# Graph attention with layer norm: another order for the last blocks' normalisation, and a flag read without its bounds check

## The chip, the cores and the metric

The kernel runs on one core of one Trainium2 chip. The metric is the device time of one execution in microseconds. Each time given for a kernel is the median of several executions; a profiled execution adds a trace with the start and length of every instruction, the events of every semaphore and the packets of the DMA engines.

## The reference

The inputs are x (4096 rows of 512 float32), a dense adjacency matrix adj (4096 x 4096 float32, 64 MiB), W (512 x 2048: four heads of 512 columns) and a (4 heads x 1024). The reference computes (`h` is x, `N` is 4096)

```python
ht = (h @ W).reshape(N, N_HEADS, N_HIDDEN).transpose(1, 0, 2)
src = jnp.einsum('hnd,hd->hn', ht, a_src)
dst = jnp.einsum('hnd,hd->hn', ht, a_dst)
e = jax.nn.leaky_relu(src[:, :, None] + dst[:, None, :], SLOPE) + adj_mat[None]
att = jax.nn.softmax(e, axis=-1)
h_prime = jnp.einsum('hij,hjd->hid', att, ht)
return h_prime.mean(axis=0)
...
x = _layernorm(x + _L0_gnn_ref(x, adj, L0_gnn_W, L0_gnn_a), axis=-1)
```

The entries of adj that are not zero are uniform up to 1e9, so the largest entry of a row outweighs all others in the softmax: the attention of row i is 1 at the column of the largest adj value and 0 elsewhere. The result for that row is then layernorm(x[i] + x[j] @ mean over heads of W), with j that column.

## The kernel before, in words

The kernel takes that short way for all rows (`leading_rows`), counts the rows for which a bound doesn't prove that the short way is exact, and branches to a full computation (`general`) where the count is above zero. On these inputs the branch is not taken.

**Tiling.** The 4096 rows are 32 blocks of 128 (`NB = 32`, blocks 0 to 31). With `Q = 4`, `LATE` is 28 and `BEHIND` is 24, so `LATE - 1` is block 27, and `NB - 3`, `NB - 2`, `NB - 1` are 29, 30 and 31. For each block SyncE's queue loads 2 MiB of adj into one of six buffers. VectorE reduces it to maxima of segments of 16 or 32 columns (L169), finds the largest segment (L176, L178), GpSimd fetches that segment again by an indirect DMA (L191), VectorE finds the place in it (L214), and GpSimd gathers the row of x with that number (L202). TensorE turns the gathered block (L229), ScalarE copies it out of PSUM into `yt` (L231, `turn`), and TensorE multiplies with the mean of W's heads (L244, `products`).

**Normalisation.** There are two ways. Blocks 0 to 26 use ScalarE and GpSimd: `stats` makes mean and sum of squares with two ScalarE passes (L266, L268), `rstd` makes the factors with three small GpSimd instructions (L271 to L273), and `finish` applies them on ScalarE (L277). Blocks 27 to 31 use VectorE: `moments` (L297, L301, and a square root on ScalarE, L303), `factor` (a reciprocal on VectorE, L306, and with `shift` one instruction more, L308), and `normalise` (L313) on VectorE; block 27 is applied by `finish` on ScalarE, and block 31 half by VectorE and half by ScalarE.

**Blocks 24 to 27** have their x loaded late. Their product is put aside by ScalarE (`put_by`) in one adj buffer, and x is added later by `add_x`: on GpSimd for 24, 25 and 26, on VectorE for 27.

**Order.** The schedule is written out by hand: each engine runs its instructions in the order of the Python calls. The loop over `t` does the 32 blocks; everything after the loop (L479 to L542) is the tail that the change touches. Stores are issued there, all on SyncE's queue, in the order in which the code names them: SyncE waits for the block of each store before it issues it, and then goes to the next. The sixteen stores use eight DMA semaphores in turn. The last six are 28, 29, the pair 24 and 25, the pair 26 and 27, 30, and 31 (L540 to L542). Stored blocks are 256 KiB each.

**The end.** `report` writes the number of unproven rows to `any_bad`; every engine loads it into a register (L63), and branches (L64). SyncE does so after its last store, and there two instructions more belong to L63: FUSED_REGOPS and SEQ_ASSERT, the check of the value against its bounds. After the branch SyncE waits for the semaphores of all engines and DMAs (L691), the last store's among them, and the program ends.

Of the kernel before, what the change touches and what calls it, by code (L numbers as in the profile page):

```python
# [27 lines left out]
@with_exitstack  # L28
def gat_resnorm_kernel(
    ctx: ExitStack,  # L30
    tc: tile.TileContext,
    x: bass.AP,
    adj: bass.AP,
    W: bass.AP,
    a: bass.AP,
    out: bass.AP,
):

    nc = tc.nc
    N, D = x.shape
    H = a.shape[0]
    KB = D // P  # L50
    NB = N // P

    ctx.enter_context(tc.manual_schedule())

    keep = ctx.enter_context(tc.tile_pool(name="keep", bufs=1))
    ident = keep.tile([P, P], F32, name="ident")
    v = keep.tile([P, KB, 2 * H], F32, name="v")
    n_bad = keep.tile([1, NB], I32, name="n_bad")
    any_bad = keep.tile([1, 1], I32, name="any_bad")

    leading_rows(tc, x, adj, W, a, out, ident, v, n_bad, any_bad)

    flag = nc.values_load(any_bad[0:1, 0:1], min_val=0, max_val=N)  # L63
    with tc.If(flag > 0, preferred_fallthrough_block=True, label="general"):  # L64
        general(tc, x, adj, W, out, ident, v, n_bad)

# [2 lines left out]
def leading_rows(ctx, tc, x, adj, W, a, out, ident, v, n_bad, any_bad):  # L69
# [8 lines left out]
    nc = tc.nc  # L78
    N, D = x.shape
    H = a.shape[0]  # L80
    KB, NB, S = D // P, N // P, N // E
# [4 lines left out]
    LATE = NB - Q  # L86
    BEHIND = LATE - Q
# [6 lines left out]
    rows = ctx.enter_context(tc.tile_pool(name="rows", bufs=2))  # L94
# [112 lines left out]
    def find_inner(ib):  # L207
        nc.vector.max(out=inner[:, ib, :], in_=lead_of[ib])
# [30 lines left out]
    def products(ib, lo=0, hi=KB):  # L239
        start = ib not in o_ps  # L240
        if start:
            o_ps[ib] = psum.tile([P, D], F32, name="o")
        for kb in range(lo, hi):
            nc.tensor.matmul(  # L244
                o_ps[ib], yt_of[ib][:, kb, :], w_sum[:, kb, :],
                start=(start and kb == 0), stop=(kb == KB - 1),
            )
# [11 lines left out]
    def add_x(engine, ib):  # L259
        o = o_ps[ib] = o_ps["by"][:, ib - BEHIND, :]  # L260
        engine.tensor_add(o, o, hold[:, ib, :])

    def stats(ib):
        o, i = o_ps[ib], slice(ib, ib + 1)
        sq = rows.tile([P, D], F32, name="sq")
        nc.scalar.activation(sq, o, AF.Identity, scale=-1.0 / D, accum_out=nm[:, i])  # L266
        sq = rows.tile([P, D], F32, name="sq")
        nc.scalar.activation(sq, o, AF.Square, bias=nm[:, i], accum_out=sd[:, i])  # L268

    def rstd(i):  # L270
        nc.gpsimd.tensor_scalar(sd[:, i], sd[:, i], 1.0 / D, EPS, op0=OP.mult, op1=OP.add)  # L271
        nc.gpsimd.tensor_tensor(sd[:, i], sd[:, i], power[:, : i.stop - i.start], op=OP.pow)  # L272
        nc.gpsimd.tensor_mul(nm[:, i], nm[:, i], sd[:, i])  # L273

    def finish(ib):
        i = slice(ib, ib + 1)
        nc.scalar.activation(hold[:, ib, :], o_ps.pop(ib), AF.Identity, bias=nm[:, i], scale=sd[:, i])  # L277
# [6 lines left out]
    def products_of_half(ib, k):  # L284
        for kb in range(KB):
            nc.tensor.matmul(  # L286
                o_ps[ib][k], yt_of[ib][:, kb, :], w_sum[:, kb, ts(k, D // 2)],
                start=False, stop=(kb == KB - 1),
            )
# [3 lines left out]
    def moments(ib):  # L293

        if ib < NB - 1:
            st = small.tile([P, nc.vector.BN_STATS_DIM], F32, name="st", bufs=2)
            nc.vector.bn_stats(st, o_ps[ib])  # L297
        else:
            st = halves_st
        mv = mean_var[ib] = small.tile([P, nc.vector.BN_AGGR_DIM], F32, name="mv", bufs=3)  # L300
        nc.vector.bn_aggr(mv, st)  # L301
        r = rt[ib] = sd[:, ib : ib + 1]
        nc.scalar.activation(r, mv[:, 1:2], AF.Sqrt, bias=eps)  # L303

    def factor(ib, shift=False):
        nc.vector.reciprocal(rt[ib], rt[ib])  # L306
        if shift:
            nc.vector.scalar_tensor_tensor(  # L308
                nm[:, ib : ib + 1], mean_var[ib][:, 0:1], -1.0, rt[ib], op0=OP.mult, op1=OP.mult
            )  # L310

    def normalise(ib, o, columns=slice(0, D)):
        nc.vector.tensor_scalar(  # L313
            hold[:, ib, columns], o, mean_var[ib][:, 0:1], rt[ib], op0=OP.subtract, op1=OP.mult
        )
# [3 lines left out]
    def stats_of_half(ib, k):  # L319
        nc.vector.bn_stats(halves_st[:, k, :], o_ps[ib][k])  # L320

    def finish_in_halves(ib):

        halves, i = o_ps.pop(ib), slice(ib, ib + 1)
        normalise(ib, halves[0], slice(0, D // 2))
        nc.scalar.activation(hold[:, ib, D // 2 :], halves[1], AF.Identity, bias=nm[:, i], scale=sd[:, i])

    def store(queue, lo, n):
        queue.dma_start(out_rows[:, ds(lo, n), :], hold[:, ds(lo, n), :])
# [82 lines left out]
    def report(pg):  # L412
        nc.vector.tensor_scalar(n_bad, pg, -1.0, float(P), op0=OP.mult, op1=OP.add)
        total = once.tile([1, 1], F32, name="total")
        nc.vector.tensor_reduce(total, pg, axis=AX.X, op=OP.add)
        nc.vector.tensor_scalar(any_bad, total, -1.0, float(N), op0=OP.mult, op1=OP.add)
# [6 lines left out]
    for t in range(NB):  # L423
# [29 lines left out]
        ib = t - PROJECT  # L453
# [48 lines left out]
    stats(BEHIND + 1)  # L502
    factor(LATE)
    normalise(LATE, o_ps.pop(LATE))
    for ib in range(BEHIND, NB):
        find_inner(ib)
    bound(3)
    test()
    turn(NB - 2)
    stats(BEHIND + 2)  # L510
    rstd(slice(BEHIND, BEHIND + 3))
    products(NB - 3, KB - 1, KB)
    pg = count()
    products(NB - 2, 0, KB - 1)
    report(pg)
    moments(NB - 3)
    factor(NB - 3)
    normalise(NB - 3, o_ps.pop(NB - 3))
    turn(NB - 1)
    products(NB - 2, KB - 1, KB)  # L520
    add_x(nc.vector, LATE - 1)
    finish(BEHIND)
    finish(BEHIND + 1)
    moments(LATE - 1)
    finish(BEHIND + 2)
    products_of_half(NB - 1, 0)
    products_of_half(NB - 1, 1)
    nc.vector.tensor_add(hold[:, NB - 2, :], o_ps[NB - 2], hold[:, NB - 2, :])
    o_ps[NB - 2] = hold[:, NB - 2, :]
    moments(NB - 2)  # L530
    factor(LATE - 1, shift=True)
    finish(LATE - 1)
    stats_of_half(NB - 1, 0)
    factor(NB - 2)
    normalise(NB - 2, o_ps.pop(NB - 2))
# [1 line left out]
    moments(NB - 1)  # L537
    factor(NB - 1, shift=True)
    finish_in_halves(NB - 1)
    for ib, n in ((NB - 4, 1), (NB - 3, 1), (BEHIND, 2), (BEHIND + 2, 2), (NB - 2, 1)):  # L540
        store(nc.sync, ib, n)
    store(nc.sync, NB - 1, 1)  # L542

# [152 lines left out]
```

## Time and profile before

| | us |
|---|---|
| median of the three runs shown | 235.62 (235.44 to 236.22) |
| the profiled execution, its own time | 236.22 |
| its span in the trace | 234.7 |
| VectorE busy | 192.2 (82%) |
| TensorE busy | 200.7 (86%) |
| ScalarE busy | 111.7 (48%) |
| GpSimd busy | 100.7 (43%) |
| mean rate of all DMA | 414 GB/s, 97.06 MB |

The profiled execution is the slowest of the three, and 1.5 us of its time lie outside the span. Times within the trace are counted from the start of the span. A line of the timeline gives start, length, engine, source line, operation and shapes, and in brackets how long the engine was idle ahead of it and what ended that. A line of the chain gives start, length and what the end of the program waited for. A line of the windows gives the stretch, its length, then the busy time and number of instructions of TensorE, its weight loads, VectorE, ScalarE and GpSimd, the granted clock, the mean busy share of the core's sixteen DMA engines, and the rate of all of them.

The tail of the trace, in the order of the code (start of each, us):

| block | statistics done | applied | store issued |
|---|---|---|---|
| 28 | 216.28 | 216.98 to 217.79 | 218.20 |
| 29 | 221.42 | 221.98 to 222.79 | 222.82 |
| 24, 25 | 218.21 | 224.61 to 226.13 | 226.16 |
| 26 | 221.09 | 226.22 to 227.02 | 227.94, with 27 |
| 27 | 224.34 | 227.11 to 227.91 | 227.94, with 26 |
| 30 | 226.63 | 227.44 to 227.99 | 228.36 |
| 31 | 229.20 | 229.84 to 230.52 | 230.54 |

### The profile page before, as it was taken

The numbers are of one execution on the slowest core, as the hardware profiler recorded it, in microseconds if no ns is written. First come the engines' busy times: TensorE is split into PE (matmuls) and PEld (weight loads), VectorE is DVE, ScalarE is ACT, GpSimd is POOL, SyncE is SP. The second block draws the span as 40 slices with busy tenths as digits, with TensorE's granted clock in tenths as the row PEclk, the third lists the DMA queues.
The fourth block names the chain that finished last, engine by engine and source line by source line (L and its number), as shares of the span: only waits on it lengthen the run. The fifth ranks groups of instructions, "written<-read, shape, count | busy, mean of one in ns | idle before, by whom it ended". The sixth has DMA issues, their size and how long they took to land.

```text
span 234.7 us, 2494 instructions
## 1 busy us (share of the span) xinstructions
PE 200.7 (86%) x683; PEld 103.0 (44%) x683; DVE 192.2 (82%) x302; ACT 111.7 (48%) x267; POOL 100.7 (43%) x212
## 2 busy tenths in 40 slices
PE   0099859999999999999969979789987988999980
PEld 0034514765656555555525424244433442444360
DVE  2726975669969996999689998998699999989871
ACT  2002112255574647474747464646464555187561
POOL 2022142414626463546444555564364554457400
PEclk9999877999999999999997999979997999999998
DMA  6999999999999999999999999999999999999994
GB/s 233 423 409 430 431 429 415 430 426 425 431 431 421 426 428 428 438 418 436 421 437 431 419 434 422 434 417 435 422 436 413 422 426 423 413 425 420 414 374 197
DMA packets 13697, 97.06 MB, mean 414 GB/s; under 512 B 2152, under 2 KB 2664, under 8 KB 7792
## 3 DMA queue, kind: packets, MB, share of 16 engines
q1 hardware_dynamic: 10080, 88.08, 89.0%
q0 software_dynamic: 3584, 8.77, 9.5%
q8 instruction: 6, 0.10, 0.2%
q14 instruction: 11, 0.09, 0.1%
q10 hardware_dynamic: 16, 0.02, 0.0%
HBM read 88.47 MB, written 8.39 MB: 413 GB/s over the span
## 4 chain that ended last, share of the span: by engine, by line
DMA 48%; POOL 19%; issue 17%; DVE 11%; PE 2%; ACT 0%; POOLq 0%; SPq 0%; DVEq 0%
DMA adj_t<-in_adj_dram 42%; DVE seg L169 8%; POOL y L202 6%; POOL lead L191 5%; DMA y<-in_x_dram,col 3%; DMA lead<-in_adj_dram,row 2%; POOL sd L272 2%; PE o L286 2%; DVE col L222 1%; POOL row L185 1%; POOL start L198 1%; POOL col L216 1%; POOL lead_early L191 1%; DVE at L178 1%; DVE top L176 1%
## 5 line engine op out<-in xcount | busy, mean ns | idle before, releaser
L169 DVE TENSOR_REDUCE seg<-adj_t 128x128 f32<-128x2048 f32 (+3 forms) x68 | 145.9, 2148 | 29.5 <-DMA adj_t<-in_adj_dram 29.4
L244 PE MATMUL o<-w_sum,yt 128*128 128x512 f32 x248 | 116.8, 612 | 0.7 <-ACT yt L231 0.7
L244 PEld LDWEIGHTS o<-w_sum,yt 128*128 128x128 f32 x248 | 45.6, 195 | 55.7 <-issue 44.4
L231 ACT COPY yt<-tp 128x512 f32<-128x512 f32 x32 | 18.8, 588 | 44.4 <-PE tp L229 44.3
L202 POOL DMA_INDIRECT y<-in_x_dram,col x32 | 30.9, 964 | 16.5 <-POOL col L216 15.8
L334 PE MATMUL o<-hold,ident 128*128 128x512 f32 x32 | 21.1, 822 | 15.1 <-POOL row L185 11.5
L237 PE MATMUL o<-hold,ident 128*128 128x512 f32 x52 | 29.0, 645 | 0.0
L229 PE MATMUL tp<-ident,y 128*128 128x128 f32 x128 | 20.0, 280 | 9.2 <-DMA y<-in_x_dram,col 9.1
L185 POOL TENSOR_TENSOR row<-at,first 128x1 uint32<-128x1 uint32 x32 | 6.1, 190 | 43.9 <-DVE at L178 43.6
L229 PEld LDWEIGHTS tp<-ident,y 128*128 128x128 f32 x128 | 14.8, 142 | 21.9 <-issue 20.3
L352 ACT COPY wt<-tp 128x512 f32<-128x512 f32 x16 | 9.2, 587 | 31.5 <-PE tp L350 31.5
L191 POOL DMA_INDIRECT lead_early<-in_adj_dram,row x18 | 18.2, 1010 | 8.8 <-POOL row L185 8.8
L216 POOL TENSOR_TENSOR col<-start,within 128x1 uint32<-128x1 uint32 x31 | 5.9, 189 | 36.5 <-DVE within L214 36.5
L251 ACT ACTIVATE sq<-hold 128x512 f32<-128x512 f32 x32 | 19.8, 619 | 0.0
L358 PEld LDWEIGHTS pv<-at_d,wt 128*128 128x128 f32 x128 | 16.3, 191 | 6.8 <-ACT wt L352 3.7
L334 PEld LDWEIGHTS o<-hold,ident 128*128 128x128 f32 x32 | 8.0, 260 | 25.7 <-POOL row L185 11.5
L335 ACT ACTIVATE w_sum<-o 128x512 f32<-128x512 f32 x4 | 2.4, 598 | 33.6 <-PE o L334 33.6
L277 ACT ACTIVATE hold<-o,nm,sd 128x512 f32<-128x512 f32 x24 | 17.2, 771 | 0.0
L191 POOL DMA_INDIRECT lead<-in_adj_dram,row x14 | 14.1, 1006 | 6.9 <-POOL row L185 6.9
L268 ACT ACTIVATE sq<-o,nm 128x512 f32<-128x512 f32 x24 | 16.5, 688 | 0.8
L358 PE MATMUL pv<-at_d,wt 128*128 128x2 f32 x128 | 15.3, 244 | 0.6 <-ACT wt L352 0.6
L266 ACT ACTIVATE sq<-o 128x512 f32<-128x512 f32 x24 | 14.6, 608 | 0.0
(91 smaller groups left out, 151.4 us busy)
## 6 DMA issues: line engine op xcount, KB each, us to landing
adj_t<-in_adj_dram SPq DMA_DIRECT2D x27, 2048.0 KB
hold<-in_x_dram SPq DMA_DIRECT2D x7, 1024.0 KB
adj_t<-in_adj_dram SPq DMA_DIRECT2D x6, 1024.0 KB
out_dram<-hold SPq DMA_DIRECT2D x10, 512.0 KB
adj_t<-in_adj_dram SPq DMA_DIRECT2D x8, 512.0 KB
hold<-in_L_gnn_W_dram SPq DMA_DIRECT2D x4, 1024.0 KB
out_dram<-hold SPq DMA_DIRECT2D x2, 1024.0 KB
hold<-in_x_dram SPq DMA_DIRECT2D x2, 512.0 KB
```

The costliest lines, as they stand in the source:

```text
L169: nc.vector.tensor_reduce(seg_of[ib][:, ts(k, N // e // n)], adj_t[ib][:, ts(k, N // n)].rearrange("p (s e) -> p s e", e=e), axis=AX.X, op ...
L191: nc.gpsimd.indirect_dma_start(out=lead, out_offset=None, in_=adj_segs_early if early else adj_segs, in_offset=bass.IndirectOffsetOnAxis(a ...
L202: nc.gpsimd.indirect_dma_start(out=y, out_offset=None, in_=x, in_offset=bass.IndirectOffsetOnAxis(ap=col[:, :1], axis=0),)
L229: nc.tensor.transpose(tp[:, kb, :], y[:, ts(kb, P)], ident)
L231: nc.scalar.copy(yt, tp)
L237: nc.tensor.matmul(o_ps[ib], ident, hold[:, ib, :], start=start, stop=False)
L244: nc.tensor.matmul(o_ps[ib], yt_of[ib][:, kb, :], w_sum[:, kb, :], start=(start and kb == 0), stop=(kb == KB - 1),)
L251: nc.scalar.activation(sq, hold[:, ib, :], AF.Square, accum_out=xx[:, ib : ib + 1])
L268: nc.scalar.activation(sq, o, AF.Square, bias=nm[:, i], accum_out=sd[:, i])
L277: nc.scalar.activation(hold[:, ib, :], o_ps.pop(ib), AF.Identity, bias=nm[:, i], scale=sd[:, i])
L334: nc.tensor.matmul(o, ident, hold[:, w_at + kb * H + h, :], start=(h == 0), stop=(h == H - 1))
L358: nc.tensor.matmul(pv[:, kb, h : 2 * H : H], wt[:, k, :], at_d[:, k, h : 2 * H : H], start=(k == 0), stop=(k == KB - 1),)
```

## The change

The flag is read with `skip_runtime_bounds_check_because`, so that FUSED_REGOPS and SEQ_ASSERT go. In the tail, the factors of 24 and 25 (`rstd`) get three GpSimd instructions of their own, issued ahead of 26's; `finish` of 24 and 25 comes ahead of 29's square root on ScalarE, `finish` of 26 behind that root, and all of it ahead of the copy of 31's turned rows. On VectorE, 27 gets its x and its moments ahead of 29's `factor` and `normalise`, and its own `factor` right behind them; `finish` of 27 comes right behind 31's copy. The pair 24 and 25 is stored ahead of 29.

```diff
-    flag = nc.values_load(any_bad[0:1, 0:1], min_val=0, max_val=N)
+    flag = nc.values_load(
+        any_bad[0:1, 0:1], min_val=0, max_val=N,
+        skip_runtime_bounds_check_because="it is N less a count of at most N rows, and only compared with zero",
+    )
...
     normalise(LATE, o_ps.pop(LATE))
+    rstd(slice(BEHIND, BEHIND + 2))
     for ib in range(BEHIND, NB):
         find_inner(ib)
     bound(3)
     test()
     turn(NB - 2)
     stats(BEHIND + 2)
-    rstd(slice(BEHIND, BEHIND + 3))
+    rstd(slice(BEHIND + 2, BEHIND + 3))
     products(NB - 3, KB - 1, KB)
     pg = count()
     products(NB - 2, 0, KB - 1)
     report(pg)
+    finish(BEHIND)
+    finish(BEHIND + 1)
     moments(NB - 3)
+    finish(BEHIND + 2)
+    add_x(nc.vector, LATE - 1)
+    moments(LATE - 1)
     factor(NB - 3)
     normalise(NB - 3, o_ps.pop(NB - 3))
     turn(NB - 1)
     products(NB - 2, KB - 1, KB)
-    add_x(nc.vector, LATE - 1)
-    finish(BEHIND)
-    finish(BEHIND + 1)
-    moments(LATE - 1)
-    finish(BEHIND + 2)
     products_of_half(NB - 1, 0)
     products_of_half(NB - 1, 1)
+    factor(LATE - 1, shift=True)
+    finish(LATE - 1)
     nc.vector.tensor_add(hold[:, NB - 2, :], o_ps[NB - 2], hold[:, NB - 2, :])
     o_ps[NB - 2] = hold[:, NB - 2, :]
     moments(NB - 2)
-    factor(LATE - 1, shift=True)
-    finish(LATE - 1)
     stats_of_half(NB - 1, 0)
...
-    for ib, n in ((NB - 4, 1), (NB - 3, 1), (BEHIND, 2), (BEHIND + 2, 2), (NB - 2, 1)):
+    for ib, n in ((NB - 4, 1), (BEHIND, 2), (NB - 3, 1), (BEHIND + 2, 2), (NB - 2, 1)):
         store(nc.sync, ib, n)
```

## The prediction

> **What bounds the kernel now.** I read the page's slices first. The sixteen DMA engines are busy in every slice but the first and the last, so the kernel is bound by bytes moved, and an order of the tail can gain only what the last slices lose.
>
> ```profile
> span 234.7 us, 2494 instructions
> ...
> DMA  6999999999999999999999999999999999999994
> GB/s 233 423 409 430 431 429 415 430 426 425 431 431 421 426 428 428 438 418 436 421 437 431 419 434 422 434 417 435 422 436 413 422 426 423 413 425 420 414 374 197
> ...
> q8 instruction: 6, 0.10, 0.2%
> ```
>
> Second, the chain of waits over the tail. What ends the compute is 31's gather, which lands at 223.33 after 7.2 us, then its transposes, its products (3.55 us), and half a block's moments and normalisation, ending at 230.52. None of these is a store or a normalisation of 24 to 27.
>
> ```profile
> 216.13 7.20 DMA y<-in_x_dram,col
> ...
> 223.47 0.63 PE tp L229 x4
> ...
> 224.95 3.55 PE o L286 x16
> ...
> 228.53 0.44 DVE halves_st L320
> ...
> 229.96 0.56 ACT hold L326
> ```
>
> Third, SyncE's own waits from 220 us on: what it waits for at the very end.
>
> ```profile
> SPq L329 <- DVE hold L313: 5.0, 2, 3.4
> ...
> SPq L691 <- DMA out_dram<-hold: 0.9, 1, 0.9
> ```
>
> The last wait is on the last store: SyncE comes to it at about 232.8 and goes on at 233.74. The store was issued at 230.54. Fourth, what moves in the meantime, in windows of half a microsecond:
>
> ```profile
> 230.50:231.00 0.50, 0.00 (x0) 0.00 (x0) 0.00 (x0) 0.02 (x1) 0.00 (x0) 1.00 0.62 238
> 231.00:231.50 0.50, 0.00 (x0) 0.00 (x0) 0.00 (x0) 0.00 (x0) 0.00 (x0) 1.00 0.41 160
> 231.50:232.00 0.50, 0.00 (x0) 0.00 (x0) 0.00 (x0) 0.00 (x0) 0.00 (x0) 1.00 1.02 397
> 232.00:232.50 0.50, 0.00 (x0) 0.00 (x0) 0.00 (x0) 0.00 (x0) 0.00 (x0) 0.98 0.22 78
> 232.50:233.00 0.50, 0.00 (x0) 0.00 (x0) 0.00 (x0) 0.00 (x0) 0.00 (x0) 0.50 0.06 25
> ```
>
> The last two columns are the DMA share and the rate. At full load sixteen engines move some 421 GB/s, 26 each; 25 GB/s with a share of 0.06 is one engine working alone. The others ran dry between 230.5 and 231.5 and were done with the last store at 232.2. The semaphore events say the same: of the last store's sixteen increments fifteen come from 232.38 to 232.70, the sixteenth at 233.72; of block 30's, fifteen by 231.82 and one at 232.80. By the packets this late engine closes its share of a store at 228.00, 228.65, 229.29, 230.54, 231.79, 232.43 and 233.08: 0.65 us for a store of 256 KiB, 1.25 for one of 512, with nothing between. It never waits for a store to be issued, it has a backlog. So the program's end is that one engine's queue, and the compute is ahead of it: the other engines began 31's packets at 231.38, 0.83 us after the issue, the late one at 232.44. The compute chain could be 1.06 us later at no cost.
>
> **The change part by part.** Sums are against the profiled execution (span 234.7, own time 236.22). It is the slowest of the three runs; the median is 0.60 lower, and I carry the difference over to it.
>
> ScalarE. After 26's statistics it has 2.4 us of wait around one square root:
>
> ```profile
> 220.90 0.19 ACT L268 ACTIVATION_READ_ACCUMULATOR sq<-adj_t,nm 128x1 f32 x1
> 221.46 0.29 ACT L303 ACTIVATE sd<-mv,eps 128x1 f32<-128x1 f32 x1 [0.37 <-DVE mv L301]
> 224.13 0.59 ACT L231 COPY yt<-tp 128x512 f32<-128x512 f32 x1 [2.38 <-PE tp L229]
> 224.61 1.52 ACT L277 ACTIVATE hold<-adj_t,nm,sd 128x512 f32<-128x512 f32 x2
> ```
>
> After the change: `finish` of 24 and 25 from 221.0 to 222.5 (the pair's 1.52), 29's root to 222.7, `finish` of 26 to 223.4 (0.80), 27's root to 223.6 (0.28, issued 0.2 after). 31's copy can then start at 223.5; its transposes let it start at 224.13. What is queued behind the new work is that copy, and TensorE's last sixteen products wait for it; cover 0.6 us. `finish` of 27 follows the copy, 224.6 to 225.4.
>
> GpSimd. The split factors are three instructions more: 0.19 + 0.72 + 0.20, with gaps 1.3 us. 24's and 25's run from 218.4 (end of 26's x) to 219.7, hidden in GpSimd's wait of 2.8 us for 26's statistics. 26's still start at 221.18 and end by 222.5, ahead of their `finish`. Nothing else is queued behind them but the flag.
>
> VectorE. 29's moments end at 221.42; 27's x (0.68), moments (0.69 + 0.18) then run to 223.06 where 29's reciprocal (0.16) and normalisation (0.81) were; these end at 224.1 instead of 222.79, and 27's factors (0.16 + 0.16) at 224.4.
>
> ```profile
> 222.71 0.68 DVE L261 TENSOR_TENSOR adj_t<-adj_t,hold 128x512 f32<-128x512 f32 x1
> 223.43 0.69 DVE L297 BATCH_NORM_STATS2 st<-adj_t 128x6 f32<-128x512 f32 x1
> 224.99 0.69 DVE L528 TENSOR_TENSOR hold<-o,hold 128x512 f32<-128x512 f32 x1 [0.66 <-PE o L244]
> ```
>
> Block 30's addition waits for TensorE until 224.99 as before: 0.5 us of cover are left. Behind it 27's two factor instructions are gone, some 0.26, so 30 is normalised at 227.85 instead of 227.99, with half of 31 still ending on TensorE at 228.50. The chain to 230.52 doesn't move: 0.
>
> SyncE's stores. 24 and 25 go out at 222.5 instead of 226.16, 29 at 224.1 instead of 222.82 (it stands behind the pair now), 26 and 27 at 225.4 instead of 227.94, 30 at 227.9 instead of 228.36, 31 at 230.54. The eight store semaphores are free in time: the last one to be used again was released at 225.94. Fifteen engines lose their idle time near 226.5 and 228.5 (slices of 0.74 and 0.83 busy) and gain it before 31's packets come, since those start no earlier than 230.54 + 0.83. The late engine has the same bytes in another order and no gap to lose: 0.
>
> The check. From the end of SyncE's load of the flag (231.43) to its branch (231.80) are 0.37 us; on ScalarE the same step takes 0.06. So 0.31 us go, and SyncE waits 1.2 us for the last store instead of 0.9: 0 as long as the late engine ends it. If the engine weren't late, the bound from the other side is the 0.31.
>
> Sum: 0, between 0 and -0.3 for the check; I take -0.1, as the late engine is what this trace shows. 235.62 - 0.1 = 235.5.
>
> The Trainium skill, "DMA: Bandwidth & Descriptors", section "Anatomy of one DMA", gives a DMA 2.0 us fixed and bytes at 436 GB/s from its issue. Worked out from that page, an estimate: the last store would land 2.6 us after its issue, at 233.15, where the trace has 233.72, and a copy of 31 held up by 0.5 us would cost 0.5 us in full; by the late engine's row it costs nothing. The same page, section "Why a DMA increments its semaphore by 16 and not by 1", has a transfer done only when all its engines are, which is what the sixteenth increment shows here and speaks against any gain from earlier issue.
>
> **The rivals.** *Faster: the late engine is not late.* Its lag of about 1.0 us (233.72 against 232.70) is not in the kernel's order of work. The trace's six 16 KiB instruction packets took about 1.0 us each, and after one at 201.8 to 202.8 a segment's sixteenth increment comes 0.83 late. If other code places such packets otherwise, the last store lands at 232.70, and SyncE, now without the check, comes to it at 232.5. End 1.0 us earlier: 234.6. For: the runs differ by 0.8 us, so something of that size comes and goes. Against: TensorE's code, the largest stream, isn't touched. Chance 0.29.
>
> *Slower: the late engine gets later.* One more instruction packet on it, in place of the one that took 226.56 to 227.58 on another engine, adds its 1.0 us, since that engine has no gap before 233.08. It decides from 0.7 us upward, which is 0.3%: 236.6. For: GpSimd's and SyncE's instruction counts change, and backlogs are deeper. Against: in this trace that packet fell elsewhere. Chance 0.15.
>
> *ScalarE holds 31's copy.* 27's root now stands in front of it, and needs VectorE's moments of 27. If VectorE's addition for 27 had to wait until `finish` of 26 has read the same adj buffer (223.4), the moments end at 225.1, the root at 225.4, the copy starts 1.3 us late and the store at 231.87. Less the 1.06 of slack: +0.26, 235.9. It decides from 1.75 us of delay on. Against: GpSimd's addition for 24 began at 209.53, before ScalarE had put 27 into that buffer at 210.00, so blocks in it don't wait for each other. Chance 0.06, mostly within 0.3%.
>
> **How the numbers follow.** The forecast, no change beyond 0.3 us, has 0.50. About 0.3%, 0.7 us, is what a measurement of this kernel can tell from no change. Faster: 0.29. Slower: 0.15 and 0.01 of the third rival. Same: 0.50 and 0.05. The range takes in both outer cases at their price, 234.5 to 236.6; beyond it are about half of each, for their own spread. The likeliest case alone is 235.0 to 236.0.
>
> **What would show it.** Right: ScalarE's three `finish` lie between 221.0 and 223.5, 31's copy starts within 0.1 us of its transposes, the pair 24 and 25 is issued near 222.5, the DMA share has no dip at 226.5, SyncE's last wait on the store is 1.2 us, and one engine still works alone at the end at 25 GB/s. Wrong: that lone stretch is missing or longer (a rival on the late engine), or the copy waits for ScalarE. The prediction fails most easily where unprofiled runs have no late engine, or another one.

## The result, and the profile after

The changed kernel takes 236.29 us, the median of 22 executions (235.88 to 237.38), against 235.69 us of the kernel before in 22 executions beside it (235.25 to 236.57). The ratio is 1.0026 with a 95% interval of [1.0013, 1.0038]: slower by some 0.6 us. The forecast was no change, 235.5 us. The range that went with it, 234.5 to 236.6, holds the measured time only because it took in the price of the slower rival; the interval of the ratio excludes no change.

The profiled execution of the changed kernel has a time of 236.16 us of its own and a span of 234.62, next to 236.22 and 234.67 before. The spans hide the difference: the 22 executions scatter by 1.3 us before and 1.5 after, and the one profiled before was among its slower ones. The tails have to be laid against an event inside them. Times are us from the span's start.

| | before | after | after less before |
|---|---|---|---|
| 31's gathered rows land | 223.33 | 222.76 | -0.57 |
| compute ends | 230.52 | 229.95 | -0.57 |
| 31's store issued | 230.54 | 229.97 | -0.57 |
| late engine closes its share of 30's store | 232.43 | 231.85 | -0.58 |
| late engine closes its share of 31's store | 233.08 | 233.19 | +0.11 |
| 31's store has landed | 233.72 | 233.65 | -0.07 |
| span ends | 234.67 | 234.62 | -0.05 |

The whole tail began 0.57 us earlier, and all of this had gone between two marks of the late engine, its closing of 30's store and its closing of 31's. First the page of the changed kernel: the span, the DMA engines' busy share in 40 slices, the rate in these slices, and the queue that carries most instruction packets.

```profile
span 234.6 us, 2495 instructions
...
DMA  6999999999999999999999999999999999999993
GB/s 228 434 423 422 440 429 432 426 427 416 436 426 421 430 433 422 430 430 432 427 432 429 426 430 427 417 429 426 433 419 422 427 426 423 413 423 420 415 419 127
...
q14 instruction: 11, 0.09, 0.1%
```

The slice before the last went from 374 to 419 GB/s, and the last one from 197 to 127. The early stores moved bytes forward by one slice, as meant. Then the chain of waits (start, length, what the end waited for):

```profile
215.66 7.10 DMA y<-in_x_dram,col
...
222.89 0.63 PE tp L232 x4
...
224.38 3.55 PE o L289 x16
...
227.95 0.44 DVE halves_st L323
...
229.38 0.56 ACT hold L329
```

It has the same steps with the same lengths; from 31's transposes to the end of compute it takes 7.05 us in both. The compute chain isn't where the time went. Next, SyncE's waits on stores at the end (us in total, number of waits, the longest), and the last windows (columns as in the windows before: clock, DMA share and rate are the last three).

```profile
SPq L695 <- DMA out_dram<-hold: 1.8, 2, 1.2
```

```profile
231.50:232.00 0.50, 0.00 (x0) 0.00 (x0) 0.00 (x0) 0.00 (x0) 0.00 (x0) 0.50 0.16 62
232.00:232.50 0.50, 0.00 (x0) 0.00 (x0) 0.00 (x0) 0.00 (x0) 0.00 (x0) 0.50 0.05 8
232.50:233.00 0.50, 0.00 (x0) 0.00 (x0) 0.00 (x0) 0.00 (x0) 0.00 (x0) 0.50 0.06 16
233.00:233.50 0.50, 0.00 (x0) 0.00 (x0) 0.00 (x0) 0.00 (x0) 0.00 (x0) 0.50 0.02 8
```

One engine still works alone, but no longer at 25 GB/s: a share of 0.05 to 0.06, so it is busy nearly all the time, and only 8 to 16 GB/s of data. The packets say what it does. The trace doesn't name the engine of a packet; the late engine's are told by each beginning where the one before ends. Right after it closes 30's store at 231.85 it takes an 8 KiB instruction packet (231.86 to 232.17), and only then 31's eight packets, the first three of which take 162, 268 and 226 ns instead of 84. Before, an instruction packet of this size stood behind its last write, at 233.09 to 233.40. So the last store took 1.34 us on this engine instead of 0.65, +0.69. Behind the last write the packet had not been free either: from write to semaphore event it took 0.64 us there and 0.47 now, -0.17. Together +0.52 us; the medians differ by 0.60. Why the packets behind the code are slow no run shows. In the profile of e11 below, the three behind TensorE's 16 KiB packet are slow as well (258, 288 and 165 ns).

Whose packet is it? After the flag is read, every engine branches, and code is fetched behind the branch: without the branch there are four instruction packets fewer (e6 below). These are the loads of the flag and VectorE's branch, listed by source line (line, engine, operation, count, duration in ns as minimum, median and maximum, first and last start), before:

```profile
L63 DVEq TENSOR_LOAD <-any_bad x1: 811/811/811, 229.8 to 229.8; - x1
L63 ACTq TENSOR_LOAD <-any_bad x1: 689/689/689, 230.0 to 230.0; - x1
...
L64 DVEq COMPARE_BRANCH  x1: 84/84/84, 230.7 to 230.7; - x1
```

and after:

```profile
L63 DVEq TENSOR_LOAD <-any_bad x1: 537/537/537, 229.2 to 229.2; - x1
L63 ACTq TENSOR_LOAD <-any_bad x1: 475/475/475, 229.4 to 229.4; - x1
...
L67 DVEq COMPARE_BRANCH  x1: 84/84/84, 229.8 to 229.8; - x1
```

The loads became shorter by 0.27 and 0.21 us, and with them VectorE's branch went from 0.12 us behind the issue of 31's store to 0.15 ahead of it. The start of the load has no part in that: it lies 0.77 us ahead of the issue in both. The load runs while the DMA engines carry the last stores, and these windows differ. Before:

```profile
229.00:229.50 0.50, 0.00 (x0) 0.00 (x0) 0.20 (x1) 0.26 (x1) 0.00 (x0) 1.00 1.03 422
229.50:230.00 0.50, 0.00 (x0) 0.00 (x0) 0.40 (x3) 0.07 (x2) 0.00 (x0) 1.00 0.99 410
```

After:

```profile
229.00:229.50 0.50, 0.00 (x0) 0.00 (x0) 0.47 (x3) 0.12 (x1) 0.00 (x0) 1.00 0.67 270
229.50:230.00 0.50, 0.00 (x0) 0.00 (x0) 0.30 (x1) 0.45 (x1) 0.00 (x0) 1.00 0.63 234
```

With the stores gone out early, the engines run dry ahead of the last one. The theory that stands at the end of this study is the chain of these readings: early stores leave the DMA engines partly idle from 229.0 on, VectorE's flag load gets shorter, its branch passes the issue of the last store, and its code goes ahead of that store on the one engine that ends the program. It was the third theory, not the first. The links from the branch to the end are tested below; that the load is shorter because the engines are partly idle is inferred from loads and windows alone.

### The profile page after: what moved, and what is told of

It reads as the page before. It is cut to its first block, busy times and chain, and to the rows that moved or that the text cites. A ratio compares the mean times of both kernels' runs of the same rounds, so it can differ in the third digit from the quotient of the medians.

```text
span 234.6 us, 2495 instructions
## 1 busy us (share of the span) xinstructions
PE 195.1 (83%) x683; PEld 100.7 (43%) x683; DVE 192.4 (82%) x302; ACT 111.8 (48%) x267; POOL 101.6 (43%) x215
## 4 chain that ended last, share of the span: by engine, by line
DMA 47%; POOL 19%; issue 18%; DVE 11%; PE 2%; ACT 0%; POOLq 0%; SPq 0%; DVEq 0%
DMA adj_t<-in_adj_dram 42%; DVE seg L172 8%; POOL y L205 6%; POOL lead L194 5%; DMA y<-in_x_dram,col 3%; DMA lead<-in_adj_dram,row 2%; POOL sd L275 2%; PE o L289 2%; DVE col L225 1%; POOL row L188 1%; POOL start L201 1%; POOL col L219 1%; POOL lead_early L194 1%; DVE at L181 1%; DVE top L179 1%
## 5 line engine op out<-in xcount | busy, mean ns | idle before, releaser
L247 PEld LDWEIGHTS o<-w_sum,yt 128*128 128x128 f32 x248 | 44.7, 193 | 54.0 <-issue 42.4
L337 PE MATMUL o<-hold,ident 128*128 128x512 f32 x32 | 18.2, 722 | 16.1 <-DMA hold<-in_L_gnn_W_dram 16.1
L240 PE MATMUL o<-hold,ident 128*128 128x512 f32 x52 | 26.8, 601 | 0.2 <-DMA hold<-in_x_dram 0.2
L337 PEld LDWEIGHTS o<-hold,ident 128*128 128x128 f32 x32 | 7.2, 237 | 24.8 <-issue 19.2
```

Of the source, the lines that this page charges most:

```text
L240: nc.tensor.matmul(o_ps[ib], ident, hold[:, ib, :], start=start, stop=False)
L247: nc.tensor.matmul(o_ps[ib], yt_of[ib][:, kb, :], w_sum[:, kb, :], start=(start and kb == 0), stop=(kb == KB - 1),)
L337: nc.tensor.matmul(o, ident, hold[:, w_at + kb * H + h, :], start=(h == 0), stop=(h == H - 1))
```

## The experiments

Unless a diff says otherwise, "changed" is the kernel after and "before" the kernel before. The table has for each run the median, that of the kernel before on the same chip, and the ratio with its interval. From each run's profile come VectorE's branch against the issue of 31's store in us (minus is ahead of it), where its code packet stands to that store on the late engine, and how long the last store took there. In e5 no engine ends alone, and the last column is empty.

| run | us | before, us | ratio | branch | code | last store |
|---|---|---|---|---|---|---|
| kernel before | 235.69 | | 1 | +0.12 | behind | 0.65 |
| kernel after | 236.29 | 235.69 | 1.0026 [1.0013, 1.0038] | -0.15 | ahead | 1.34 |
| e1_check_only | 235.38 | 235.38 | 1.0006 [0.9996, 1.0017] | +0.12 | behind | 0.65 |
| e2_order_only | 236.09 | 235.38 | 1.0027 [1.0014, 1.0041] | -0.15 | ahead | 1.23 |
| e3_old_store_order | 236.49 | 235.38 | 1.0043 [1.0023, 1.0062] | -0.16 | ahead | 1.33 |
| e4_before_again | 235.71 | 235.38 | 1.0015 [0.9999, 1.0030] | +0.13 | behind | 0.65 |
| e5_late_stores | 235.71 | 235.67 | 0.9995 [0.9980, 1.0011] | +0.45 | behind | |
| e6_before_no_branch | 235.14 | 235.67 | 0.9977 [0.9964, 0.9990] | none | none | 0.65 |
| e7_changed_no_branch | 235.06 | 235.67 | 0.9976 [0.9964, 0.9989] | none | none | 0.65 |
| e8_pair_only_early | 235.84 | 235.67 | 0.9998 [0.9984, 1.0012] | +0.05 | behind | 0.65 |
| e9_changed_held | 240.16 | 235.38 | 1.0208 [1.0179, 1.0237] | +0.63 | behind | 0.65 |
| e10_before_held | 240.48 | 235.38 | 1.0207 [1.0180, 1.0234] | +0.64 | behind | 0.65 |
| e11_before_tensor_late | 235.53 | 235.38 | 0.9999 [0.9986, 1.0011] | +0.11 | behind | 0.65 |
| e12_changed_vector_held | 240.02 | 235.38 | 1.0191 [1.0166, 1.0215] | +0.63 | behind | 0.65 |
| e13_held | 235.72 | 235.68 | 0.9998 [0.9988, 1.0008] | +0.63 | behind | 0.64 |
| e14_before_held | 235.84 | 235.68 | 1.0006 [0.9994, 1.0017] | +0.63 | behind | 0.65 |
| e15_vector_held | 235.90 | 235.68 | 1.0010 [0.9997, 1.0023] | +0.64 | behind | 0.65 |
| e16_scalar_held | 236.12 | 235.68 | 1.0020 [1.0008, 1.0031] | -0.16 | ahead | 1.34 |
| e17_changed_long_hold | 235.47 | 235.64 | 0.9993 [0.9981, 1.0005] | +1.84 | behind | 0.64 |
| e18_before_long_hold | 235.51 | 235.64 | 0.9998 [0.9984, 1.0012] | +1.84 | behind | 0.65 |

### Which part of the change

The first theory was that SyncE's branch does it. Without the check it comes 0.96 us behind the issue of 31's store instead of 1.26, and code behind it could reach the late engine sooner. The rivals were the new order of work, and the place of 29's store in it. The change was taken apart. e1_check_only is the kernel before with the check left out alone, e2_order_only the changed one with the check put back (the diff is e2's, against the changed kernel):

```diff
-    flag = nc.values_load(
-        any_bad[0:1, 0:1], min_val=0, max_val=N,
-        skip_runtime_bounds_check_because="it is N less ...",
-    )
+    flag = nc.values_load(any_bad[0:1, 0:1], min_val=0, max_val=N)
```

> The kernel before with one edit: the flag is read without its bounds check. Theory 'code packet' (SyncE branches 0.3 us sooner, so an 8 KiB instruction packet of about 0.3 us, which came behind the last store's data on the late DMA engine in the profile of before, at 233.09, now comes ahead of it, as at 231.61 in the profile of the changed kernel): slower by 0.2 to 0.3%, 236.2 to 236.4, and the last store lands 3.6 us or more after its issue (3.20 before). Theory 'deep backlog' (the early stores of 24 to 27 are what delays the engines that fetch code): no change within 0.1%, last store 3.2 us after its issue or less. Theory 'luck' (nothing but the run's spread): no change.

> The changed kernel with the bounds check back: all of the reordering, FUSED_REGOPS and SEQ_ASSERT kept. Theory 'code packet': as before, within 0.1%, last store 3.2 us after its issue. Theory 'deep backlog': slower by 0.2 to 0.3%, TensorE's 16 KiB code packet again some 3 us behind its branch (0.7 us in the profile of before, 3.3 us in that of the changed kernel), and the last store 3.6 us or more after its issue.

e3_old_store_order is the changed kernel with the pair 24 and 25 stored behind 29 again:

```diff
-    for ib, n in ((NB - 4, 1), (BEHIND, 2), (NB - 3, 1), (BEHIND + 2, 2), (NB - 2, 1)):
+    for ib, n in ((NB - 4, 1), (NB - 3, 1), (BEHIND, 2), (BEHIND + 2, 2), (NB - 2, 1)):
```

> The changed kernel with the stores in the order of before: 29 ahead of the pair 24 and 25, so that 29 (ready near 223.4) holds up the pair (ready near 222.0) by 1.4 us; nothing else differs from the changed kernel. If putting 29 behind the pair is the cause: as fast as before. 'Code packet': slower by 0.2 to 0.3%, like the changed kernel. 'Deep backlog': slower like the changed kernel, or a little less (the queue is 1.4 us shorter at 222, and as deep from 225 on).

e4_before_again is the kernel before without an edit, to see how it varies.

> The kernel before without any edit, for its spread and a second profile. All theories: ratio 1.000 within 0.1%. Its executions lie in two groups, near 235.5 and near 236.4; the profile of before was in the upper group (236.22). If the late DMA engine makes the groups, a profile of the lower group has its last store landing 0.7 us sooner after its issue than 3.20, and SyncE's last wait is under 0.3 us.

The check's removal is worth nothing either way (1.0006), and the order alone is as slow as the whole change (1.0027). The first theory falls: in e2 SyncE branches 1.26 us behind the issue of 31's store, as in the kernel before, and it is slow all the same; in e1 it branches 0.96 us behind it, as in the changed kernel, and nothing is lost. The order of 29 and the pair isn't the cause (1.0043, with an interval that reaches down to the whole change's). e4 is the same program as the kernel before, and its ratio is 1.0015 [0.9999, 1.0030], so single ratios closer to 1 than that say little. Its profile, of an execution of 235.48 us, had the last store land 3.34 us after its issue, not sooner than the 3.18 in the one of 236.22; but 31's rows had landed 0.90 us earlier (222.43 against 223.33). Between these two executions the difference was made ahead of the tail, and not by the late engine.

### Early stores, and the branch

The second theory was that the early stores leave another backlog, in which TensorE's 16 KiB packet comes at 228.70 to 229.66 instead of 226.56 to 227.58, and that one of these packets delays the end. Its rival was the new order of compute itself. e5_late_stores keeps the changed compute and stores late:

```diff
-    for ib, n in ((NB - 4, 1), (BEHIND, 2), (NB - 3, 1), (BEHIND + 2, 2), (NB - 2, 1)):
+    for ib, n in ((NB - 4, 1), (NB - 3, 1), (NB - 2, 1), (BEHIND, 2), (BEHIND + 2, 2)):
```

> The changed kernel, all compute in its new order, but the stores of 24 to 27 named behind 30: SyncE waits for 30 (ready near 227.3) and issues 30, the two pairs and 31 from there on, so the DMA engines run dry near 226 as they do in the kernel before. Theory 'deep backlog': back to the time of before within 0.15% (or up to 0.1% slower for the dry stretch), TensorE's 16 KiB code packet again about 1 us behind its branch. Theory 'compute order' (ScalarE's, VectorE's or GpSimd's new order itself costs): slower by 0.2 to 0.3% like the changed kernel.

e6_before_no_branch and e7_changed_no_branch leave the flag's load, the branch and the full computation behind it out of the kernel before and of the changed one (the diff is e6's):

```diff
-    flag = nc.values_load(any_bad[0:1, 0:1], min_val=0, max_val=N)
-    with tc.If(flag > 0, preferred_fallthrough_block=True, label="general"):
-        general(tc, x, adj, W, out, ident, v, n_bad)
...
-        if t == NB // 2:
-            tc.mark_branch_hint_location("general", engines=HINTED)
```

> The kernel before without the flag, the branch and the full computation (left out: the path for rows that the short way doesn't prove, which these inputs never take); no engine has to fetch code behind a branch. It is the base for the next run. Theory 'code packet behind the backlog': faster than before by 0.1 to 0.5% (no 16 KiB packet on a DMA engine near the end, no load of the flag ahead of the last waits).

> The changed kernel with the same things left out. Theory 'code packet behind the backlog' (the reordering costs because TensorE's code packet, held back by the deeper backlog, makes its engine late for the last stores): as fast as the kernel before without branch, or faster by up to 0.1%. Theory 'backlog by itself' (deeper store queues delay the last store whatever the code does): slower than it by 0.2 to 0.3%.

e8_pair_only_early is the kernel before with the split factors, `finish` of 24 and 25 early, and the pair stored ahead of 29; 26 and 27 stay late.

```diff
+    rstd(slice(BEHIND, BEHIND + 2))
...
-    rstd(slice(BEHIND, BEHIND + 3))
+    rstd(slice(BEHIND + 2, BEHIND + 3))
...
+    finish(BEHIND)
+    finish(BEHIND + 1)
     moments(NB - 3)
...
-    finish(BEHIND)
-    finish(BEHIND + 1)
     moments(LATE - 1)
...
-    for ib, n in ((NB - 4, 1), (NB - 3, 1), (BEHIND, 2), (BEHIND + 2, 2), (NB - 2, 1)):
+    for ib, n in ((NB - 4, 1), (BEHIND, 2), (NB - 3, 1), (BEHIND + 2, 2), (NB - 2, 1)):
```

> The kernel before with a third of the reordering: factors and normalisation of 24 and 25 early and their store ahead of 29's; 26, 27 and the check as before. Theory 'deep backlog': the dry stretch at 226.5 is filled, that at 228.5 stays, so the packet falls near 228 and the cost is between none and that of the change, 0 to 0.2% slower. Theory 'compute order', in VectorE's part of it (27 ahead of 29): no change.

The changed compute with late stores costs nothing (0.9995). Without the branch both kernels take the same time (0.9977 and 0.9976), so the early stores cost nothing by themselves either. The loss needs both: early stores and the branch. The page of e6_before_no_branch shows what went with the branch:

```profile
q8 instruction: 5, 0.08, 0.1%
q14 instruction: 8, 0.07, 0.1%
```

One packet fewer on the queue of the 16 KiB packets (6 with the branch) and three fewer on the other (11 with it): that fits one each for the four engines that the kernel names in `HINTED`, TensorE, ScalarE, VectorE and GpSimd; SyncE isn't among them. With them go 0.23% of the time, 0.53 us, from a branch that is never taken. Of these, 0.30 us are seen at the last store, whose event follows its last write by 0.34 us instead of 0.64. The edit takes the loads of the flag away too, and no view shows where the rest lies. The Trainium skill, "Runtime: NRT & Kernel Launch", section "Instruction fetch mechanics", calls the cost of crossing into the next block of code mostly hidden; here the fetch comes with a branch and shares a DMA engine with the last store, and these 0.30 us are not hidden.

Storing the pair alone early is harmless (0.9998). There VectorE's load of the flag takes 0.75 us, its branch falls 0.05 us behind the issue, and its code behind the last write.

### TensorE's packet, or VectorE's

Two of the branch's packets were left as suspects: TensorE's, which moved by 2 us, and one of 8 KiB. e11_before_tensor_late gives the kernel before TensorE's late packet, by a small product that has to wait for block 30:

```diff
+    late = psum.tile([1, NB], F32, name="px", bufs=1)
+    nc.tensor.matmul(late, ones[:, 0:1], hold[:, NB - 2, :NB], start=True, stop=True)
     for ib, n in ((NB - 4, 1), (NB - 3, 1), (BEHIND, 2), (BEHIND + 2, 2), (NB - 2, 1)):
```

> The kernel before with one small matmul more at the end of TensorE that reads block 30 once it is normalised (near 228.0), so that TensorE branches near 228.8 instead of 225.4 and its 16 KiB code packet comes at 229 to 230 instead of 226.6, in a full queue. Theory 'TensorE's 16 KiB packet': slower by 0.2 to 0.4%, as in the changed kernel. Theory 'code of VectorE and ScalarE overtakes the last store': no change within 0.12%, as the packet hits an engine that isn't the late one.

TensorE branched at 228.38, its packet came at 230.97 to 231.93, later than in the changed kernel, and the time didn't move (0.9999). The second theory, which I had favoured, falls in its half on TensorE. It was a near thing: in this profile the packets behind TensorE's were slow, and their engine was the last to end 31's store, at 233.51, 0.09 us behind the engine with VectorE's code.

The same runs were to hold back the branches of VectorE and ScalarE, by a copy that reads block 31 on each ahead of the flag's load, in the changed kernel (e9_changed_held) and in the one before (e10_before_held), and on VectorE alone in the changed one (e12_changed_vector_held, without the last line):

```diff
+    held = once.tile([P, 2], F32, name="held")
+    nc.vector.tensor_copy(held[:, 0:1], hold[:, NB - 1, D - 1 : D])
+    nc.scalar.copy(held[:, 1:2], hold[:, NB - 1, 0:1])
```

> The changed kernel, with one small copy more at the end of VectorE and of ScalarE, each of which waits for the other's last half block, so that both engines read the flag and branch some 0.3 to 0.6 us later. In the profiles so far they read it in 0.47 to 0.54 us where the stores are early (DMA engines dry by 229) and in 0.69 to 0.82 where they are late, so that they branch 0.05 to 0.15 us ahead of the last store's issue instead of 0.05 to 0.2 behind it, and an 8 KiB code packet then stands ahead of the last store on the late DMA engine instead of behind it. Theory 'code of VectorE and ScalarE overtakes the last store': back to the time of before, within 0.12%. Theory 'TensorE's 16 KiB packet at 228.7' (instead of 226.5): still slower by 0.2 to 0.4%.

> The kernel before with the same two copies: what they cost by themselves. Both theories: no change within 0.1%, since the branch of both engines is a microsecond ahead of the last store's landing.

> The changed kernel with VectorE's copy alone: VectorE branches later, ScalarE 0.05 us ahead of the last store as in the changed kernel. If VectorE's code is what stands ahead of the last store on the late engine: back to the time of before. If it is ScalarE's: slower by 0.2 to 0.3% like the changed kernel. If TensorE's packet is the cause: slower as well.

All three lost some 5 us, the kernel before too, and their times said nothing on the question; their profiles have VectorE's code behind the last write, as wanted. What did it was not the copies, which e14 below has at no cost, but the new tile of 8 bytes per partition. It presumably moves what lies behind it in SBUF; no view shows addresses. The rate in the slices of e10_before_held is lower all along the main loop, mostly between 403 and 426 GB/s where the kernel before had 409 to 438:

```profile
GB/s 236 436 431 421 424 432 411 429 420 403 426 420 418 406 420 431 416 410 425 411 423 425 414 421 421 412 410 418 421 416 414 407 412 415 399 418 421 416 406 190
```

### VectorE's code ahead of the last store

The experiment was made again with existing tiles (`gap`, `xx`) that nobody needs by then. e13_held is the changed kernel with both copies, e14_before_held the one before with both, e15_vector_held and e16_scalar_held the changed one with the first or the second alone:

```diff
+    nc.vector.tensor_copy(gap[:, 0:1], hold[:, NB - 1, D - 1 : D])
+    nc.scalar.copy(xx[:, 0:1], hold[:, NB - 1, 0:1])
     for ib, n in ((NB - 4, 1), (BEHIND, 2), (NB - 3, 1), (BEHIND + 2, 2), (NB - 2, 1)):
```

> As e9, but the two copies go into columns of gap and xx, which nothing reads any more, so that no tile is added and SBUF is laid out as before. VectorE and ScalarE branch 0.4 to 0.6 us behind the last store's issue. Theory 'code overtakes the last store': within 0.12% of the kernel before, the code packet on the late engine right behind its last write. If the packet's place doesn't matter: still 0.2 to 0.4% slower.

> The kernel before with the same two copies into gap and xx. Theory 'code overtakes the last store': no change within 0.1%, as its packet is behind the last store already. It also tells whether the 2% of e9, e10 and e12 are the added tile: if so, nothing of them is left here.

> The changed kernel with VectorE's copy alone (into gap). In the profile of e12 the packet at the late engine came right behind its last write (3.32 us after the issue) and another one at 1.65: so VectorE's code is the one on the late engine. Expected then: within 0.12% of before. If it was ScalarE's: 0.2 to 0.4% slower.

> The changed kernel with ScalarE's copy alone (into xx). If VectorE's code is the one on the late engine: 0.2 to 0.4% slower, like the changed kernel. If it was ScalarE's: within 0.12% of before.

With both copies the loss is gone (0.9998 [0.9988, 1.0008], clear of the change's 1.0026 [1.0013, 1.0038]), and the kernel before isn't moved by them (1.0006). VectorE's load and branch, and the last windows, of e13_held:

```profile
L63 DVEq TENSOR_LOAD <-any_bad x1: 536/536/536, 230.8 to 230.8; - x1
...
L67 DVEq COMPARE_BRANCH  x1: 84/84/84, 231.4 to 231.4; - x1
```

```profile
232.50:233.00 0.50, 0.00 (x0) 0.00 (x0) 0.00 (x0) 0.00 (x0) 0.00 (x0) 1.00 0.06 25
233.00:233.50 0.50, 0.00 (x0) 0.00 (x0) 0.00 (x0) 0.00 (x0) 0.00 (x0) 1.00 0.08 33
```

The load is as short as in the changed kernel, 0.54 us, but it starts after the last store's issue at 230.81, and the lone engine is back at 25 GB/s. The same two views of e16_scalar_held, which holds ScalarE alone and issues 31's store at 229.81:

```profile
L63 DVEq TENSOR_LOAD <-any_bad x1: 536/536/536, 229.0 to 229.0; - x1
...
L67 DVEq COMPARE_BRANCH  x1: 84/84/84, 229.7 to 229.7; - x1
```

```profile
231.50:232.00 0.50, 0.00 (x0) 0.00 (x0) 0.00 (x0) 0.00 (x0) 0.00 (x0) 1.00 0.06 25
232.00:232.50 0.50, 0.00 (x0) 0.00 (x0) 0.00 (x0) 0.00 (x0) 0.00 (x0) 1.00 0.08 12
232.50:233.00 0.50, 0.00 (x0) 0.00 (x0) 0.00 (x0) 0.00 (x0) 0.00 (x0) 0.72 0.05 20
```

VectorE branches 0.16 us ahead of the issue, the code is taken ahead of the store (231.70 to 232.01), and the engine drops to 12 GB/s. e15_vector_held has it the other way round: VectorE 0.64 behind, ScalarE still 0.04 ahead, the code behind the last write and 0.65 us for the last store. With 31's store issued at 230.32, its two branches are

```profile
L67 ACTq COMPARE_BRANCH  x1: 68/68/68, 230.3 to 230.3; - x1
L67 DVEq COMPARE_BRANCH  x1: 84/84/84, 231.0 to 231.0; - x1
```

So the packet is VectorE's. The ratios, 1.0010 for e15 and 1.0020 for e16, point the same way, but their intervals overlap; between these two the verdict rests on the profiles and on the last column of the table, where 0.64 or 0.65 goes with "behind" or no code and 1.23 to 1.34 with "ahead" in every run that has an entry. In e5 all engines are backed up to the end, and none is alone. Leaving aside the three kernels with the new tile, the four with the code ahead have ratios of 1.0020 to 1.0043, the ten with it behind 0.9993 to 1.0015.

### Can the packet be kept out altogether

Behind the last write the packet still costs some 0.3 us between write and event. A longer hold should let the event go first: VectorE reads two blocks again, ScalarE copies a column of the result and VectorE copies it back, all ahead of the flag's load. e17_changed_long_hold does this in the changed kernel, e18_before_long_hold in the one before:

```diff
+    nc.vector.tensor_reduce(gap[:, 0:1], hold[:, BEHIND : BEHIND + 2, :], axis=AX.XY, op=OP.max)
+    nc.scalar.copy(xx[:, 0:1], gap[:, 0:1])
+    nc.vector.tensor_copy(gap[:, 1:2], xx[:, 0:1])
```

> The changed kernel with VectorE and ScalarE held longer: VectorE reduces two stored blocks into gap (some 1.2 us), ScalarE copies that, VectorE copies it again, so that both read the flag about 1.4 us after the last store's issue and branch at 2.0. Their code packets then come behind the last store's semaphore write. Theory: the last increment follows its write by 0.36 instead of 0.64 us, 0.1% (0.05 to 0.15%) faster than before. If the packet behind the write costs nothing, or the held engines end later than SyncE's last wait: no change, or slower by up to 0.1%.

> The kernel before with the same hold. Theory: as e17, 0.05 to 0.15% faster than before; and no difference between the two orders, as without the branch (e6 and e7).

The event then follows the write in 0.34 us instead of 0.64, and the last store lands 2.87 and 2.86 us after its issue. The medians are 0.17 and 0.13 us lower than before, and both intervals hold 1. No version that keeps the branch is shown to beat the kernel before. e17 also answers for TensorE's packet in the changed order: it comes at 228.30, 1.33 us ahead of the last store's issue, much as in the changed kernel (1.27), and nothing is lost.

## Why the prediction was wrong

*What bounds the kernel: right.* One late DMA engine ends it, and the compute has slack ahead of it. From 31's rows to the engine's closing of 30's store are 9.10 us before and 9.09 after.

*ScalarE, GpSimd, VectorE: right but for one duration.* Less the 0.57 us by which this execution was earlier, the three `finish` were to lie between 220.4 and 222.9. ScalarE's timeline of the changed kernel (start, length, line, operation) has them from 220.44 to 223.07, and 31's copy waits for the transposes, not for them:

```profile
220.44 1.50 ACT L280 ACTIVATE hold<-adj_t,nm,sd 128x512 f32<-128x512 f32 x2
221.84 0.28 ACT L306 ACTIVATE sd<-mv,eps 128x1 f32<-128x1 f32 x1
222.26 0.81 ACT L280 ACTIVATE hold<-adj_t,nm,sd 128x512 f32<-128x512 f32 x1
222.98 0.28 ACT L306 ACTIVATE sd<-mv,eps 128x1 f32<-128x1 f32 x1
223.56 0.58 ACT L234 COPY yt<-tp 128x512 f32<-128x512 f32 x1 [0.30 <-PE tp L232]
```

The copy's cover was 0.30 us rather than 0.6. 0.13 of that went to GpSimd: its power of 26's single column took 1.07 us, longer than the 0.89 of three columns in the trace of before, and `finish` of 26 could start only at 222.26. In e2 it took 0.99 us, in the other runs that have it 0.55; why, no run shows. Block 30's addition waits for TensorE until 224.42, the predicted 224.99 less 0.57.

*SyncE's stores: right* to 0.15 us. The pair goes out at 221.96, 29 at 223.42, 26 and 27 at 224.88, 30 at 227.33; the dip at 226.5 is gone, with a DMA share of 1.05 and 1.08 in the half microseconds on either side of it, and the idle time lies ahead of 31's packets, as predicted.

*The check: 0 instead of -0.1* (1.0006 [0.9996, 1.0017]). The step's zero was right and its wait wrong. SyncE comes 0.31 us sooner, but then it waits for 30's store, so that its last wait is the time between the landings of 30 and 31. With the check alone left out (e1) it has two waits, and the last is as long as before:

```profile
SPq L694 <- DMA out_dram<-hold: 1.5, 2, 0.9
```

The 1.2 us of the changed kernel are the predicted number by luck: there 31's store lands 1.2 us behind 30's (232.42, 233.65), because the late engine takes longer over it.

*"The late engine has the same bytes in another order and no gap to lose: 0": this step failed.* In place of 0 the late engine lost 0.52 us, 0.69 on the last store less 0.17 behind its last write. The bytes are the same and there was no gap, but code packets are in that order too, and I had followed the stores alone. The step before had put the idle time at the right place. What it missed is that the flag's loads run just there and that VectorE's gets 0.27 us shorter, which was enough for VectorE's branch to pass the issue of 31's store by 0.15 us. The branch appears nowhere in the working but for SyncE's.

*The rivals.* The slower one named the right place and the right kind of cause, an instruction packet on the late engine, and the wrong event: not one packet more in place of TensorE's, but VectorE's own, from behind the last write to ahead of the last store. Its price was 1.0 us, from the 16 KiB packets; the real one is +0.69 and -0.17. The faster rival, an engine that isn't late, didn't come about: in the changed kernel the late engine closes block 30's store where it did. The third didn't either.

*The estimate of 2.6 us.* The page that it is worked out from gives its 2.0 us and 436 GB/s in a section on DMAs that GpSimd issues, while 31's store is issued by SyncE. Nothing in the sum rests on them. From issue to landing the store took 3.18 us before and 3.68 after.

*What would show it.* Four of the signs came as listed, and the wait of 1.2 us came for another reason. The sixth, a lone engine at 25 GB/s, came at 8 to 16, and that number alone pointed to the cause.

## What to carry to other kernels

Where the end of a kernel is one DMA engine's queue, list everything that goes through that queue, the code behind branches too, and see on which side of the last store each packet falls. A change that moves nothing on the chain of waits can still turn that order, by making a load on another engine some tenths of a us shorter. An engine whose code comes too early can be held by an instruction that reads what the last store reads, without a new tile: here that took the ratio from 1.0026 [1.0013, 1.0038] back to 0.9998 [0.9988, 1.0008].

## What the runs showed of the hardware

- A branch that is not taken, at the end of the program, cost 0.23% with the loads of its flag (e6, 0.9977 [0.9964, 0.9990]). VectorE's 8 KiB instruction packet took 0.31 us on the late DMA engine; ahead of the last store it made this store 0.69 us longer there, behind the last write it lengthened write to event from 0.34 us (e6, e7, e17, e18) to 0.64.
- VectorE's load of one value into a register took 0.54 us where the DMA share over the load was 0.25 to 0.63 (after, e2, e3, e13 to e16), 0.75 to 0.82 at 0.98 to 1.05 (before, e1, e4, e8, e11), and 1.14 in e5, at 1.03. That the load waits behind DMA traffic is inferred from this, and it isn't the whole: under full traffic TensorE's and GpSimd's loads took 0.49 and 0.62 us in the kernel before, and ScalarE's 0.49 in e17 and e18. The Trainium skill, "DMA: Bandwidth & Descriptors", section "Latency and other measured facts", gives such a load a floor of about 600 ns; VectorE's 0.54 us goes below it.
- VectorE's code went ahead of the store when its branch was 0.15 us ahead of the store's issue, and behind it when it was 0.05 us behind (e8).
- TensorE's 16 KiB packet comes 1.1 us after its branch in the kernel before (225.44, 226.56), where the engines were 72 to 76% busy from 226.0 on, and 3.7 us after it in the changed one (224.97, 228.70), where they were full until then. In e11 it comes 2.6 us after its branch, at 230.97, and costs nothing (0.9999 [0.9986, 1.0011]).
- A new tile of 8 bytes per partition cost 2% (e10, 1.0207, against 1.0006 of the same copies without it in e14). That the place of other tiles in SBUF is the reason is not shown.
